# Pattern stage of a graph network: three settle groups instead of two, a task order by kind, candidates' rows gathered and turned, lone nodes' rows gathered per group

## The chip, the cores and the metric

The kernel runs on one core of a Trainium2 chip. TensorE (PE) does matmuls and transposes, VectorE (DVE) and ScalarE (ACT) elementwise work, GpSimd (POOL) elementwise work and the indirect gathers; SyncE (SP) issues most plain transfers. The metric is the device time of one execution in microseconds (us), lower is better. Shown is the median of three timed runs; beside them one profiled execution, from which all durations below come.

## The reference, cut to what matters

Sixteen graphs of N = 1024 nodes with F = 128 features pass four layers. Layer 0 is an attention over the nonzero entries of each graph's adjacency matrix. Layer 1 thins the adjacency first and then runs three convolutions with batch normalisation; layers 2 and 3 are dense products with the whole adjacency. Each layer adds its input and is layer-normalised. The change concerns the thinning of layer 1, which is a loop over the rows of each graph:

```python
def step(carry, n):
    row = jnp.take(carry, n, axis=0)
    nbi = row.astype(jnp.int32)
    num = jnp.sum(nbi)
    sf = jnp.where(num > T_DIL, (num + K_DIL - 1) // K_DIL, 1)   # T_DIL = 10, K_DIL = 2
    rank = jnp.cumsum(nbi)
    rm = row & (rank % sf == 0)
    valid = (mask_b[n] != 0) & (num > 1)
    rm = jnp.where(valid, rm, False)
    keep = ~rm
    carry = carry.at[n].set(row & keep)
    carry = carry.at[:, n].set(carry[:, n] & keep)
    return (carry, None)
```

A row with at most ten neighbours (when its turn comes) loses all of them; a row with more loses the neighbours whose running rank is a multiple of half their number. What is left is very sparse.

## The kernel before, in words

The program has four phases, one after the other: the attention (`phase_att`, which also writes a 0/1 copy of every adjacency to DRAM, `mask_d`, and the layer's result `x1_d`), the pattern stage (`phase_pattern`), the convolutions (`phase_conv`) and the dense layers (`phase_end`). Only the pattern stage is changed. It replaces the sequential loop by a few matmul passes. For each of the 16 graphs b it runs two generators, and for each half of the graphs a third one; a `yield` divides each into steps.

`find(b)` (L751) loads the graph's mask (2 MB, tile `m`, three buffers, L754) and counts degrees with 64 one-column matmuls (L760). POOL cuts the eight diagonal blocks of the mask (`md`, L767). Three passes `earlier` (L777, L781) tell which nodes keep nothing ("small") and which are candidates; at most 128 candidates get a slot each. `slots` (L713 to L722) makes a one-hot matrix `oh` of nodes by slots, `nodes` (L727 to L733) the node number of each slot and the index of its row in DRAM. POOL gathers the candidates' rows of the adjacency by that index (`rows`, L810: 128 rows of 4 KB). The candidates' columns of the mask come from a product of the whole mask with `oh`: `pg`, 64 matmuls of 128x128 (L823). DVE multiplies `pg` by `stay` into `base` (L831), which a further product ranks (`pr`, L837, `RB`, `num0`). Last, `rows` are transposed (L854), copied (L856) and multiplied with `oh32` (L860) into `V`.

`settle(g)` (L864) works on eight graphs at once. Five rounds follow each other, each with nine small DVE operations (128x8), three wide ones (128x1024, L896 to L898), eight one-column matmuls (L901) and a copy of their result `gone` (L903), on which the next round's first operation depends. Then follow wide operations, three products and a transpose, and a store to `slots_d` (L953).

`alone(b)` (L956) ranks all nodes of one graph against its settled candidates (`prank`, L964), marks hits on ACT and DVE (L970, L972), finds the nodes that are left alone, gives them slots as above, and issues two gathers on POOL: the candidates' rows of x1 (L989, through `rows_of_x1`, L746) and the lone nodes' diagonal entries (L990). After all tasks, `rows_of_x1` gathers the lone nodes' rows of x1 for all 16 graphs (L1006), for which `inner` (L735) makes the indices per half.

`rolling(tasks, 5, 2)` (L635, L1003) interleaves the generators in program order: at most five are active, a new one starts when the last one has made two steps, and only the head of the list may start:

```python
while (todo and len(active) < depth and (not active or active[-1][2] >= lag)
       and all(n in ended for n in todo[0][2])):
```

The list is f0 to f9, s0, then f10, a0, f11, a1 and so on to f15, a5, then s1, a6, a7, and a8 to a15 (f for find, s for settle, a for alone). s0 needs f0 to f7, a0 to a7 need s0, s1 needs f8 to f15, a8 to a15 need s1.

Program order is not quite the order of execution: a planner places each engine's instructions ahead of time, by program order and by its own estimates of when an operand is ready. So an instruction may stand earlier than the program has it (the trace has flag operations of L1024, written after all tasks, at 1708 us). [...]

PSUM holds two wide buffers (tag `pb`, shared by `pg`, `pt`, `py`, `pk`, `prank`) and four small ones (tag `ps`).

Of the kernel before, what the change touches and what calls it, by code (L numbers as in the profile page):

```python
# [10 lines left out]
F32 = mybir.dt.float32  # L11
F32R = mybir.dt.float32r
BF16 = mybir.dt.bfloat16
F16 = mybir.dt.float16
# [3 lines left out]
ALU = mybir.AluOpType  # L18
# [4 lines left out]
B, N, F = 16, 1024, 128  # L23
P = 128
T = N // P
# [75 lines left out]
EDGE = 256.0  # L101
# [512 lines left out]

KEEP = 10
ROUNDS = 5
HALF = B // 2


# [12 lines left out]
    arrays["q_one_up"] = np.ascontiguousarray(np.broadcast_to(node[:P], (P, P)))  # L632


def rolling(tasks, depth, lag):  # L635


    todo, active, ended = list(tasks), [], set()
    while todo or active:
        while (  # L640
            todo and len(active) < depth and (not active or active[-1][2] >= lag)
            and all(n in ended for n in todo[0][2])
        ):
            active.append([todo[0][0], todo[0][1], 0])
            todo.pop(0)
        for a in list(active):
            try:
                next(a[1])
                a[2] += 1
            except StopIteration:  # L650
                active.remove(a)
                ended.add(a[0])
# [3 lines left out]
def phase_pattern(ctx, tc, t, c, mask_d, slots_d, x1_d, keep, flags):  # L656
# [78 lines left out]
    def inner(k0, k1):  # L735

        k = slice(k0, k1)
        at = sm.tile([P, HALF], F32, name="at")
        none = sm.tile([P, HALF], F32, name="none")
        nc.vector.tensor_scalar(at, keep.node[:, k], -1.0, 0.0, op0=ALU.add, op1=ALU.max)  # L740
        nc.vector.tensor_scalar(none, keep.node[:, k], 0.0, float(N), op0=ALU.is_equal, op1=ALU.mult)
        nc.vector.tensor_copy(keep.inner[:, k], at)
        nc.vector.tensor_tensor(keep.row[:, k], at, none, ALU.add)

    def rows_of_x1(k):
        nc.gpsimd.indirect_dma_start(  # L746
            keep.xs[:, k, :], None, x1_d[k % B],
            bass.IndirectOffsetOnAxis(ap=keep.inner[:, k : k + 1], axis=0),
        )

    def find(b):  # L751
# [60 lines left out]
            bass.IndirectOffsetOnAxis(ap=keep.index[:, b : b + 1], axis=0),  # L812
        )

        le = wp.tile([P, T, P], F16, name="le", bufs=3)
        for ti in range(T):
            nc.scalar.activation(le[:, ti, :], row, AF.Sign, bias=half_up[:, ti : ti + 1])
# [1 line left out]

        pg = ps_b.tile([P, T, P], F32, name="pg", tag="pb")  # L820
        for ni in range(T):
            for ci in range(T):
                nc.tensor.matmul(  # L823
                    pg[:, ni, :], m[:, ci, ni * P : (ni + 1) * P], oh[:, ci, :],
                    start=ci == 0, stop=ci == T - 1,
                )
        late = sm.tile([P, T], F16, name="late")
        nc.vector.scalar_tensor_tensor(late, cand, 2.0 * N, node_col, op0=ALU.mult, op1=ALU.add)
        stay = wp.tile([P, T, P], F16, name="stay")
# [33 lines left out]

    def settle(g):  # L864

        bs = slice(g * HALF, (g + 1) * HALF)
        shape = [P, HALF, P]

        def tiny(name):
            return sm.tile([P, HALF], F32, name=name, bufs=3)  # L870

        def wide(name, dtype=F16):
            return lp.tile(shape, dtype, name=name)

        def spread(x):
            return x.unsqueeze(2).to_broadcast(shape)

        gone = tiny("gone")
        nc.vector.memset(gone, 0.0)
        rb = RB[:, bs, :]  # L880
        for k in range(ROUNDS):
            num, h, big, top = tiny("num"), tiny("h"), tiny("big"), tiny("top")
            nc.vector.scalar_tensor_tensor(num, num0[:, bs], 1.0, gone, op0=ALU.add, op1=ALU.subtract)

            nc.vector.tensor_scalar(h, num, 0.5, 0.25, op0=ALU.mult, op1=ALU.add)
            nc.vector.tensor_scalar(h, h, ROUND, None, op0=ALU.add)
            nc.vector.tensor_scalar(h, h, ROUND, None, op0=ALU.subtract)
            nc.vector.tensor_scalar(big, num, float(KEEP), None, op0=ALU.is_gt)


            nc.vector.scalar_tensor_tensor(v1[:, bs], h, EDGE - 1, gone, op0=ALU.add, op1=ALU.add)
            nc.vector.tensor_tensor(top, v1[:, bs], h, ALU.add)
            nc.vector.scalar_tensor_tensor(top, top, -EDGE, big, op0=ALU.add, op1=ALU.mult)
            nc.vector.tensor_scalar(v2[:, bs], top, EDGE, None, op0=ALU.add)
            e1, e2, rm = wide("e1"), wide("e2"), wide("rm")
            nc.vector.tensor_tensor(e1, rb, spread(v1[:, bs]), ALU.is_equal)  # L896
            nc.vector.tensor_tensor(e2, rb, spread(v2[:, bs]), ALU.is_ge)
            nc.vector.tensor_tensor(rm, e1, e2, ALU.max)  # L898
            pn = ps_s.tile([P, HALF], F32, name="pn", tag="ps")
            for j in range(HALF):  # L900
                nc.tensor.matmul(pn[:, j : j + 1], rm[:, j, :], one, start=True, stop=True)  # L901
# [5 lines left out]
        inner(g * HALF, (g + 1) * HALF)  # L907
# [8 lines left out]
        for j in range(HALF):  # L916
# [15 lines left out]
        nc.vector.scalar_tensor_tensor(k1, num, 1.0, k1, op0=ALU.is_le, op1=ALU.max)  # L932
# [3 lines left out]
        for j in range(HALF):  # L936
# [12 lines left out]
        pt = ps_b.tile(shape, F32, name="pt", tag="pb")  # L949
        for j in range(HALF):  # L950
# [42 lines left out]
        )  # L993
        yield

    tasks = [(f"f{b}", find(b), []) for b in range(HALF + 2)]
    tasks.append(("s0", settle(0), [f"f{b}" for b in range(HALF)]))
    for b in range(HALF - 2):
        tasks += [(f"f{HALF + 2 + b}", find(HALF + 2 + b), []), (f"a{b}", alone(b), ["s0"])]
    tasks.append(("s1", settle(1), [f"f{b}" for b in range(HALF, B)]))  # L1000
    tasks += [(f"a{b}", alone(b), ["s0"]) for b in (HALF - 2, HALF - 1)]
    tasks += [(f"a{b}", alone(b), ["s1"]) for b in range(HALF, B)]
    rolling(tasks, 5, 2)  # L1003
    inner(B, B + HALF)
    inner(B + HALF, 2 * B)
    for k in range(B, 2 * B):  # L1006
        rows_of_x1(k)


    nc.vector.tensor_scalar(keep.lone, keep.lone, 1.0, None, op0=ALU.min)  # L1010

# [1202 lines left out]
```

## Time and profile before

| | |
|---|---|
| median of three runs | 3212.45 us (3210.42 to 3214.26) |
| profiled execution | 3201.61 us, span 3199.7 us |
| PE busy over the span | 2800.9 us (88%) |
| DVE busy | 2251.8 us (70%) |
| ACT busy | 1778.9 us (56%) |
| POOL busy | 1271.8 us (40%) |
| mean granted TensorE clock | 0.922 |
| pattern stage in the trace | about 1690 to 2083 us |

Busy time is the time in which an engine had an instruction in execution; matmul ends are modelled, so a busy PE is not a PE at its peak. The pattern stage lies between the last work of the attention (POOL's L531 at 1689.4 us) and the last product of the last `alone` (L728 at 2082.1 us). The span is cut into stretches below, with the busy time of every engine in each; in such a table the number behind an engine's busy time is its count of instructions, and PEclk is the granted clock.

### The profile page before, as it was taken

What the parts mean: (1) busy time and instruction counts of PE and PEld (TensorE: products, weight loads), DVE (VectorE), ACT (ScalarE), POOL (GpSimd) and SP (SyncE); (2) the same over time, 40 slices, a digit from 0 to 9 for tenths busy, and PEclk for the clock granted to TensorE, in tenths of its full rate; (3) what the DMA queues carried; (4) which work ended last, traced back from release to release, by engine and by line L of the source; (5) the groups of instructions that cost most, each with busy time, mean ns of one, the idle gap of its engine ahead of it and who ended that gap; (6) DMA issues with size and microseconds to landing.
All of it is one profiled execution on the core that took longest, in us unless ns stands there. A gap on an engine that the chain in (4) does not pass through costs nothing. (4 is left out here: it accounts for less than half of the span.)

```text
span 3199.7 us, 70693 instructions
## 1 busy us (share of the span) xinstructions
PE 2800.9 (88%) x25724; PEld 2487.4 (78%) x25724; DVE 2251.8 (70%) x8226; ACT 1778.9 (56%) x5608; POOL 1271.8 (40%) x1280
## 2 busy tenths in 40 slices
PE   6999999999999999999996968477786899999997
PEld 3877877778777877788886858266676899999997
DVE  5878878788788878788774466746555566666665
ACT  3867777777776777777772323145645233333342
POOL 5645555454545454453113423243423223333221
PEclk8999999999999999999996878688988899999999
DMA  6422332223322332222023532044444434444441
GB/s 179 116 66 79 85 99 79 65 79 99 92 63 80 94 99 75 69 78 72 21 92 115 188 108 93 16 161 143 149 171 151 161 130 156 174 159 168 158 146 30
DMA packets 162023, 348.62 MB, mean 109 GB/s; under 512 B 14708, under 2 KB 68230, under 8 KB 161536
## 3 DMA queue, kind: packets, MB, share of 16 engines
q1 hardware_dynamic: 149760, 311.37, 30.6%
q0 software_dynamic: 10752, 28.42, 3.1%
q10 hardware_dynamic: 1152, 4.19, 0.5%
q8 instruction: 206, 3.38, 0.4%
q14 instruction: 153, 1.25, 0.1%
HBM read 257.87 MB, written 87.03 MB: 108 GB/s over the span
## 5 line engine op out<-in xcount | busy, mean ns | idle before, releaser
L272 POOL TENSOR_SCALAR mask<-ld 104x1024 f16<-104x1024 f32 (+1 forms) x150 | 443.2, 2955 | 548.1 <-PE pw L354 236.1
L434 PE MATMUL pg<-parts,oh 104*128 104x384 f32 (+1 forms) x1760 | 539.0, 382 | 49.7 <-ACT hg L452 49.1
L465 PE MATMUL pa<-hg,we 128*104 128x129 f32 (+1 forms) x3520 | 569.4, 277 | 1.8
L446 DVE SCALAR_TENSOR_TENSOR junk<-pg,w_a 128x128 f32<-128x128 f32 x1600 | 405.2, 283 | 173.3 <-PE pg L439 170.1
L465 PEld LDWEIGHTS pa<-hg,we 128*104 128x104 f32 x3520 | 498.0, 175 | 32.8 <-ACT hg L452 19.6
L452 ACT ACTIVATE hg<-pg,hg 128x128 f32<-128x128 f32 x1600 | 509.8, 370 | 17.1
L439 PE MATMUL pg<-parts,oh 104*128 104x384 f32 (+1 forms) x1760 | 473.2, 343 | 0.0
L434 PEld LDWEIGHTS pg<-parts,oh 104*128 104x128 f32 x1760 | 282.2, 193 | 78.4 <-ACT hg L452 62.0
L439 PEld LDWEIGHTS pg<-parts,oh 104*128 104x128 f32 x1760 | 314.6, 193 | 0.0
L450 ACT ACTIVATE hg<-sc 128x2 f32<-128x2 f32 (+1 forms) x880 | 188.6, 216 | 168.6 <-DVE junk L446 163.2
L419 DVE TENSOR_TENSOR we<-k_id,ids 128x832 f32<-128x832 f16 (+1 forms) x240 | 228.5, 952 | 8.5 <-PE pa L465 4.7
L1343 POOL TENSOR_TENSOR rstd<-ve,mhalf 128x4 f32<-128x4 f32 x96 | 97.0, 1010 | 323.9 <-DVE ve L1342 323.8
L389 ACT CAST oh<-oh_b 104x1024 fp32r<-104x1024 bf16 (+1 forms) x240 | 221.3, 977 | 1.9 <-DVE oh_b L385 1.7
L291 PE MATMUL pw<-w_all,xT 128*104 128x512 f32 x320 | 185.6, 664 | 17.0 <-DMA xT<-in_xTp 8.3
L1347 DVE TENSOR_SCALAR x<-x,mv,rstd 128x128 f32<-128x128 f32 x256 | 104.7, 449 | 92.6 <-POOL rstd L1343 92.6
L385 DVE TENSOR_TENSOR oh_b<-pw,k_slot_edge 104x512 bf16<-104x512 f32 (+1 forms) x240 | 144.6, 635 | 9.6 <-PE pw L384 7.1
L357 ACT CAST qs<-pw 104x416 f16<-104x416 f32 (+1 forms) x240 | 114.4, 477 | 66.4 <-PE pw L354 62.7
L364 DVE SCALAR_TENSOR_TENSOR one_way<-qs,mask 104x1040 bf16<-104x1040 f16 (+9 forms) x160 | 150.4, 940 | 0.1
L500 POOL TENSOR_TENSOR own<-parts 104x128 f32<-104x128 f32 x160 | 96.9, 637 | 118.4 <-DVE x_rows L521 82.4
L1452 ACT ACTIVATE y<-x,shift,rstd 128x128 f32<-128x128 f32 x128 | 52.7, 482 | 162.9 <-POOL shift L1445 162.9
L378 ACT CAST oh_b<-pw 104x512 bf16<-104x512 f32 (+1 forms) x240 | 133.1, 556 | 13.6 <-PE pw L377 13.5
L336 DVE TENSOR_TENSOR g<-k_slot,off 105x1408 f16<-105x1408 f16 x80 | 131.9, 1649 | 11.5 <-ACT off L332 11.4
(356 smaller groups left out, 6662.0 us busy)
## 6 DMA issues: line engine op xcount, KB each, us to landing
ld<-in_adjT SPq DMA_DIRECT2D x135, 416.0 KB
m<-mask_d SPq DMA_DIRECT2D x16, 2048.0 KB
keep_adj<-in_adjT SPq DMA_DIRECT2D x8, 4096.0 KB
adj<-in_adjT SPq DMA_DIRECT2D x8, 4096.0 KB
mask_d<-mask SPq DMA_DIRECT2D x144, 208.0 KB
hT_d<-uT SPq DMA_DIRECT2D x48, 512.0 KB
h<-hT_d SPq DMA_DIRECT2D x48, 512.0 KB
hT<-hT_d SPq DMA_DIRECT2D x32, 512.0 KB
```

What stands on the lines that cost most here:

```text
L272: engine.tensor_scalar(mt[:n, s, :N], ld[:n], 0.0, None, op0=ALU.is_gt)
L291: nc.tensor.matmul(pw[:W], xT[:, s * W : (s + 1) * W], w_all, start=True, stop=False, skip_group_check=True)
L364: nc.vector.scalar_tensor_tensor(junk[:W, :nb, :], q[:W, at : at + nb, :W], EDGE, mt[:W, i, i * W : NP].rearrange("p (n w) -> p n w", w=W) ...
L385: nc.vector.tensor_tensor(o[:W, n0 : n0 + m, 1, :], pw[:W, :m, :], k_slot_edge[:W].unsqueeze(1).to_broadcast([W, m, C]), ALU.is_equal,)
L389: nc.scalar.copy(wide.ends[:W, n0 : n0 + m], o[:W, n0 : n0 + m])
L419: nc.vector.tensor_tensor(we[:, :n, :], k_id.unsqueeze(1).to_broadcast([P, n, W]), wide.ids[:, 2 * lo : 2 * hi].unsqueeze(2).to_broadcast( ...
L434: nc.tensor.matmul(flat[:, first : 3 * F], own, d.parts[i][:W, p, first:], start=p == 0, stop=False, skip_group_check=True,)
L439: nc.tensor.matmul(pg[:, 1::step, :], other, reversed_parts(d.parts[j][:W, p, :], step), start=False, stop=p == 1, skip_group_check=True,)
L446: nc.vector.scalar_tensor_tensor(junk, pg[:, 1 + e, :], 0.0, w_a2, op0=ALU.max, op1=ALU.mult, accum_out=d.sc[:, at + e : at + e + 1],)
L450: nc.scalar.activation(hg[:, u - lo, :ways, F], d.sc[:, at : at + ways], AF.Exp)
L452: nc.scalar.activation(hg[:, u - lo, e, :F], pg[:, 3 - 3 * e, :], AF.Copy, scale=hg[:, u - lo, e, F : F + 1])
L465: nc.tensor.matmul(PA[bank][:W, at : at + part.stop - part.start], we[:, 2 * (u - lo) + e, :], hg[:, u - lo, e, part], start=False, stop=T ...
```

## The change

Five edits, all in the pattern stage.

1. The groups of `settle` are 0 to 5, 6 to 11 and 12 to 15, where there were 0 to 7 and 8 to 15; its tiles shrink from eight to six or four graphs, and `settle` runs three times.
2. `rolling` starts tasks by kind: up to four finds, one settle and two of the kind "alone" are active at once, each kind with a lag of two steps among its own, and any task of the list whose predecessors have ended may start, not only the head.
3. The candidates' columns of the mask: a second gather on POOL fetches the candidates' rows of `mask_d` (128 rows of 2 KB, tile `marks`); `pg` becomes eight matmuls that turn them (with a diagonal matrix `there`, one small DVE operation, which also blanks unused slots). The mask is symmetric without its diagonal, so rows and columns agree.
4. The small operations of a round fall from nine to seven; one more stands after the rounds.
5. The lone nodes' rows of x1 are gathered in three tasks `lone_rows(g)`, each after the six, six or four `alone` of its group, in place of one block after all tasks.

```diff
+GROUPS = ((0, 6), (6, 12), (12, 16))
...
-def rolling(tasks, depth, lag):
+def rolling(tasks, most, lag):
...
-        while (
-            todo and len(active) < depth and (not active or active[-1][2] >= lag)
-            and all(n in ended for n in todo[0][2])
-        ):
-            active.append([todo[0][0], todo[0][1], 0])
-            todo.pop(0)
+        for task in list(todo):
+            name, kind, steps, after = task
+            same = [a for a in active if a[1] == kind]
+            if len(same) < most[kind] and (not same or same[-1][3] >= lag) and ended.issuperset(after):
+                active.append([name, kind, steps, 0])
+                todo.remove(task)
...
+        marks = wp.tile([P, N], F16, name="marks")
+        nc.gpsimd.indirect_dma_start(
+            marks, None, mask_d.rearrange("b n m -> (b n) m"),
+            bass.IndirectOffsetOnAxis(ap=keep.index[:, b : b + 1], axis=0),
+        )
+
+        there = sm.tile([P, P], F16, name="there")
+        nc.vector.tensor_scalar(there, same, keep.node[:, b : b + 1], 1.0, op0=ALU.mult, op1=ALU.min)
...
         for ni in range(T):
-            for ci in range(T):
-                nc.tensor.matmul(
-                    pg[:, ni, :], m[:, ci, ni * P : (ni + 1) * P], oh[:, ci, :],
-                    start=ci == 0, stop=ci == T - 1,
-                )
+            nc.tensor.matmul(pg[:, ni, :], marks[:, ni * P : (ni + 1) * P], there, start=True, stop=True)
...
-            nc.vector.scalar_tensor_tensor(num, num0[:, bs], 1.0, gone, op0=ALU.add, op1=ALU.subtract)
-
-            nc.vector.tensor_scalar(h, num, 0.5, 0.25, op0=ALU.mult, op1=ALU.add)
-            nc.vector.tensor_scalar(h, h, ROUND, None, op0=ALU.add)
-            nc.vector.tensor_scalar(h, h, ROUND, None, op0=ALU.subtract)
-            nc.vector.tensor_scalar(big, num, float(KEEP), None, op0=ALU.is_gt)
-
-
-            nc.vector.scalar_tensor_tensor(v1[:, bs], h, EDGE - 1, gone, op0=ALU.add, op1=ALU.add)
-            nc.vector.tensor_tensor(top, v1[:, bs], h, ALU.add)
+
+            nc.vector.scalar_tensor_tensor(num, num0[:, bs], 1.5, gone, op0=ALU.add, op1=ALU.subtract)
+            nc.vector.tensor_scalar(h, num, 0.5, ROUND, op0=ALU.mult, op1=ALU.add)
+            nc.vector.tensor_scalar(big, num, KEEP + 0.5, None, op0=ALU.is_gt)
+
+
+            nc.vector.scalar_tensor_tensor(v1[:, bs], h, EDGE - 1 - ROUND, gone, op0=ALU.add, op1=ALU.add)
+            nc.vector.scalar_tensor_tensor(top, h, -ROUND, v1[:, bs], op0=ALU.add, op1=ALU.add)
...
-    tasks = [(f"f{b}", find(b), []) for b in range(HALF + 2)]
-    tasks.append(("s0", settle(0), [f"f{b}" for b in range(HALF)]))
-    for b in range(HALF - 2):
-        tasks += [(f"f{HALF + 2 + b}", find(HALF + 2 + b), []), (f"a{b}", alone(b), ["s0"])]
-    tasks.append(("s1", settle(1), [f"f{b}" for b in range(HALF, B)]))
-    tasks += [(f"a{b}", alone(b), ["s0"]) for b in (HALF - 2, HALF - 1)]
-    tasks += [(f"a{b}", alone(b), ["s1"]) for b in range(HALF, B)]
-    rolling(tasks, 5, 2)
-    inner(B, B + HALF)
-    inner(B + HALF, 2 * B)
-    for k in range(B, 2 * B):
-        rows_of_x1(k)
-
+    def lone_rows(g):
+        b0, b1 = GROUPS[g]
+        inner(B + b0, B + b1)
+        for k in range(B + b0, B + b1):
+            rows_of_x1(k)
+        yield
+
+    tasks = [(f"f{b}", "find", find(b), []) for b in range(B)]
+    for g, (b0, b1) in enumerate(GROUPS):
+        tasks.append((f"s{g}", "settle", settle(g), [f"f{b}" for b in range(b0, b1)]))
+        tasks += [(f"a{b}", "alone", alone(b), [f"s{g}"]) for b in range(b0, b1)]
+        tasks.append((f"x{g}", "alone", lone_rows(g), [f"a{b}" for b in range(b0, b1)]))
+    rolling(tasks, {"find": 4, "settle": 1, "alone": 2}, 2)
```

The rest of the diff passes the width of the group (`b1 - b0`) where `HALF` stood, and takes the constant `ROUND` off `h` once after the rounds.

More of the change, by code (lines that the diff above doesn't have):

```diff
@@ L632, in pattern_constants @@
     arrays["q_one_up"] = np.ascontiguousarray(np.broadcast_to(node[:P], (P, P)))
-def rolling(tasks, depth, lag):
+def rolling(tasks, most, lag):
     todo, active, ended = list(tasks), [], set()
     while todo or active:
-        while (
-            todo and len(active) < depth and (not active or active[-1][2] >= lag)
-            and all(n in ended for n in todo[0][2])
-        ):
-            active.append([todo[0][0], todo[0][1], 0])
-            todo.pop(0)
+        for task in list(todo):
[4 more added lines that the diff above has]
+                todo.remove(task)
         for a in list(active):
             try:
-                next(a[1])
-                a[2] += 1
+                next(a[2])
+                a[3] += 1
             except StopIteration:
@@ L737, in inner @@
         k = slice(k0, k1)
-        at = sm.tile([P, HALF], F32, name="at")
-        none = sm.tile([P, HALF], F32, name="none")
+        at = sm.tile([P, k1 - k0], F32, name="at")
+        none = sm.tile([P, k1 - k0], F32, name="none")
         nc.vector.tensor_scalar(at, keep.node[:, k], -1.0, 0.0, op0=ALU.add, op1=ALU.max)
@@ L864, in settle @@
     def settle(g):
-        bs = slice(g * HALF, (g + 1) * HALF)
-        shape = [P, HALF, P]
+        b0, b1 = GROUPS[g]
+        bs, n = slice(b0, b1), b1 - b0
+        shape = [P, n, P]
         def tiny(name):
-            return sm.tile([P, HALF], F32, name=name, bufs=3)
+            return sm.tile([P, n], F32, name=name, bufs=3)
         def wide(name, dtype=F16):
@@ L898, in settle @@
             nc.vector.tensor_tensor(rm, e1, e2, ALU.max)
-            pn = ps_s.tile([P, HALF], F32, name="pn", tag="ps")
-            for j in range(HALF):
+            pn = ps_s.tile([P, n], F32, name="pn", tag="ps")
+            for j in range(n):
                 nc.tensor.matmul(pn[:, j : j + 1], rm[:, j, :], one, start=True, stop=True)
@@ L906, in settle @@
         nc.vector.tensor_scalar(below[:, bs], v2[:, bs], -0.5, None, op0=ALU.add)
-        inner(g * HALF, (g + 1) * HALF)
+        nc.vector.tensor_scalar(h, h, -ROUND, None, op0=ALU.add)
+        inner(b0, b1)
         up = wide("up")
@@ L915, in settle @@
         py = ps_b.tile(shape, F32, name="py", tag="pb")
-        for j in range(HALF):
+        for j in range(n):
             nc.tensor.matmul(py[:, j, :], up[:, j, :], run[:, :P], start=True, stop=True)
@@ L931, in settle @@
         nc.vector.tensor_tensor(k1, k1, big, ALU.mult)
-        nc.vector.scalar_tensor_tensor(k1, num, 1.0, k1, op0=ALU.is_le, op1=ALU.max)
+        nc.vector.scalar_tensor_tensor(k1, num, 1.5, k1, op0=ALU.is_le, op1=ALU.max)
         own = wide("own")
@@ L935, in settle @@
         pk = ps_b.tile(shape, F32, name="pk", tag="pb")
-        for j in range(HALF):
+        for j in range(n):
             nc.tensor.matmul(pk[:, j, :], same, low[:, j, :], start=True, stop=False)
@@ L949, in settle @@
         pt = ps_b.tile(shape, F32, name="pt", tag="pb")
-        for j in range(HALF):
+        for j in range(n):
             nc.tensor.transpose(pt[:, j, :], d[:, j, :], c.ident)
@@ L994, in alone @@
         yield
-    tasks = [(f"f{b}", find(b), []) for b in range(HALF + 2)]
-    tasks.append(("s0", settle(0), [f"f{b}" for b in range(HALF)]))
-    for b in range(HALF - 2):
-        tasks += [(f"f{HALF + 2 + b}", find(HALF + 2 + b), []), (f"a{b}", alone(b), ["s0"])]
-    tasks.append(("s1", settle(1), [f"f{b}" for b in range(HALF, B)]))
-    tasks += [(f"a{b}", alone(b), ["s0"]) for b in (HALF - 2, HALF - 1)]
-    tasks += [(f"a{b}", alone(b), ["s1"]) for b in range(HALF, B)]
-    rolling(tasks, 5, 2)
-    inner(B, B + HALF)
-    inner(B + HALF, 2 * B)
-    for k in range(B, 2 * B):
-        rows_of_x1(k)
+    def lone_rows(g):
+        b0, b1 = GROUPS[g]
+        inner(B + b0, B + b1)
[8 more added lines that the diff above has]
+    rolling(tasks, {"find": 4, "settle": 1, "alone": 2}, 2)
     nc.vector.tensor_scalar(keep.lone, keep.lone, 1.0, None, op0=ALU.min)
```

## The prediction

> **What bounds the kernel now.** I read the page first. The chain that ended last reaches back only to about 2379 us, behind the pattern stage, so it says nothing of it. I therefore cut the stage into stretches at the places where its character changes, and asked for the busy time of each engine:
>
> ```profile
> core 0: us, PE busy (x) PEld busy (x) DVE busy (x) ACT busy (x) POOL busy (x), PEclk, DMA share, GB/s
> 1690.00:1858.00 168.00, 140.67 (x2861) 137.02 (x2862) 77.62 (x205) 50.88 (x141) 70.87 (x122) 0.75 0.52 167
> 1858.00:1898.00 40.00, 16.04 (x279) 14.96 (x278) 33.85 (x89) 3.75 (x10) 3.73 (x9) 0.55 0.07 24
> 1898.00:1997.00 99.00, 88.38 (x1697) 80.08 (x1697) 56.56 (x143) 36.70 (x90) 29.66 (x41) 0.90 0.33 106
> 1997.00:2046.00 49.00, 16.19 (x159) 12.32 (x159) 40.10 (x114) 3.80 (x6) 12.70 (x13) 0.57 0.06 14
> 2046.00:2083.00 37.00, 23.84 (x246) 14.12 (x244) 26.33 (x68) 10.14 (x18) 7.76 (x9) 0.82 0.06 19
> 2083.00:2095.00 12.00, 3.01 (x12) 2.78 (x13) 3.21 (x15) 0.92 (x2) 8.53 (x9) 0.50 0.88 282
> ```
>
> The stage alternates between two bounds. In the first and third stretch (finds; finds with six alones) PE is busy 84% and 89%, DVE 46% and 57%. In the second and fourth (the two settles) PE is busy 40% and 33%, and DVE, at 85% and 82%, follows a chain from round to round. The fifth holds the eight last alones, the sixth the handover to the convolutions. From 1690 to 2083 (393 us) PE has 285.1 us of work and DVE 234.5: neither fills the time.
>
> Next the groups by shape from 1690 to 2100, for the operations the change touches, then that stretch's list of waits:
>
> ```profile
> L823 PE MATMUL pg<-oh,m 128*128 128x128 f16 x1024 | 67.9, 233 | 1.6 <-DVE oh L719 1.6
> L767 POOL TENSOR_TENSOR md<-m,q_less 128x128 f16<-128x128 f16 x128 | 59.7, 501 | 52.4 <-DMA m<-mask_d 52.2
> L810 POOL DMA_INDIRECT rows<-in_adj,keep_index x16 | 21.8, 1359 | 78.1 <-issue 38.9 <-PE pu L781 33.6 <-DVE keep_index L731 5.6
> ```
>
> ```profile
> POOL md L767 <- DMA m<-mask_d: 52.2, 10, 15.5
> ...
> PE pn L901 <- DVE rm L898: 36.6, 8, 6.2
> ...
> PE pt L854 <- DMA rows<-in_adj,keep_index: 14.6, 8, 3.1
> ```
>
> `pg` is PE's largest item, 67.9 us. PE waits 36.6 us for settle rounds. POOL stands 52.2 us for mask loads, because in the old kernel a mask buffer is held until `pg` has read it. The issue queue of SP shows the pitch of a find:
>
> ```profile
> 1722.72 129.36 SPq L754 DMA_DIRECT2D m<-mask_d  x10
> ```
>
> Ten loads start over 129.36 us, so 14.4 us lie between two finds. From 1858 on nothing new starts until s0 has ended: a0 heads the list and waits for it.
>
> [...] `rows` lands after a median of 4.7 us (4.3 to 6.8). [...] while `md` ran at 1862.0 to 1865.6, settle's small operations took 0.35 to 0.41 us, otherwise 0.17. [...] the settle stretches show 0.55 and 0.57, the third stretch 0.90. Filling those holes should not cost clock.
>
> **The change part by part.**
>
> *Columns by gather (edit 3).* PE loses 1024 matmuls of 67.9 us, 66 ns each in a row, and gains 128: 8.5 us. PE's work falls from 285.1 to 225.7. DVE gains 16 `there`, by the nearest rows (L689, L691: 0.18 and 0.41 us) 3 to 7 us; I take 3. POOL gains 16 gathers; `rows` takes 1.36 us on POOL, so 21.8 us, no bound beside POOL's 125 of 393 us. The DMA engines move 2.9 instead of 2.6 MB per find; at the 287 GB/s seen at 1660 to 1680 us, 10 us, below the old pitch. Gain: a mask buffer comes free after the third `earlier`, so loads start sooner and POOL's 52.2 us of waiting shrinks. The new wait: `pg` waits for a gather that waits for the node numbers. From index to landing I count 1.36 (`rows`) + 1.36 (`marks`) + 4.7 = 7.4 us; ahead of it may stand another find's `md` (59.7/16 = 3.7 us). Behind `pg` on PE stand the other finds' passes, and settle's and alone's products. One step of three other finds covers some 2.3 us of PE (a find will have 8.3 us in eleven steps, below). For `rows`, with two steps more of cover, PE waited only 14.6 us in all, as the planner put other work ahead. For `marks` I bound the loss at 0 to 5 us per find and take 1.5; part falls into time in which PE has nothing else to do.
>
> *Three groups (edits 1, 4).* The elements stay. Per settle there were about 69 small operations (45 in rounds), now 60; three times 60 against twice 69 is 42 more at 0.17, +7 us. There are 24 wide operations per settle; from 1.22 us at 1024 elements and 0.35 at 128 (L840) the fixed part is about 0.2 us, so +4 us with a third settle. DVE: 234.5 + 3 + 7 + 4 = 248.
>
> *Order by kind (edit 2).* It takes away the head of the list that blocks. Finds go on while s0 and s1 run, so DVE's settle rounds and PE's find passes lie beside each other. It moves every find's `rows` and mask load past settle, on POOL and SP; I price that as the utilisation below.
>
> *Lone rows per group (edit 5).* The last eight gathers ran at 2084 to 2094 us, 1.25 us each, beside the handover, in which PE waited 9.3 us for weights and not for them. So moving them gains nothing. The cover lost: six of them stand in POOL's queue for 7.5 us ahead of some find's gathers, two times; at worst 15 us, I take 2 inside the utilisation.
>
> *The sum.* PE per find: 140.67 us over 168/14.4 = 11.7 finds, 12.0 us; less 59.4/16 = 3.7, it is 8.3. At the 84% that PE reached in the first stretch this gives a pitch of 10 us, with the DMA's 10 us just as tight; I take 10.5. f0 ended at 1748.7 us (its `V` copy); f5 then ends near 1801. By then DVE has done about eight finds' work (six whole, four begun) at 7.8 us (the rows of one find, mean durations summed, and `there`) and 4 us of constants, 66 us. There remain 182 us, and PE's 226 - 8 x 8.3 = 160. DVE is now the larger load. If DVE is busy 80% of the rest (between the 71% of the last alones and the 89% of PE in the third stretch, near the settles' 82 and 85%), 182/0.80 = 227 us, and the stage ends at 2028 instead of 2083: 55 us less. A check on another way: even at the old pitch of 14.4 us, f15 would end at 1749 + 15 x 14.4 = 1965; a settle of four graphs (five rounds of about 3.7 us and 9 us behind them, 27 us) and four alones (37/8 = 4.6 us each, 18) bring 2010. So the overlap pays most, and DVE limits. Handover and later phases stay. The profiled execution, 3201.6 us, would become 3146.6; the median shown lies 10.8 us above it, so 3157 us.
>
> **The rivals.**
>
> *A, smaller gain.* DVE reaches only 71%, as in the fifth stretch, where it waits for ACT and PE in turns, and `marks` costs its waits. 182/0.71 = 256 us, an end at 2057, 26 us less: 3186. For it: two engines almost equally loaded and queues in a fixed order. Against it: three kinds of independent tasks.
>
> *B, larger gain.* DVE reaches PE's 89%: 204 us, an end at 2005, 78 us less: 3134. For it: that stretch had only two kinds of task and reached 89%.
>
> *C, slower.* The wait for `marks` takes the place of `pg`'s work. POOL places a later find's `md`, which waits for its mask (up to 15.5 us before), ahead of `marks`; PE stands at `pg`, and since `base` needs `pg`, DVE stands too. With 5 us uncovered in each of 16 finds that is 80 us against the 55: 25 us slower, 3237. It decides from 55/16 = 3.4 us per find in which both engines are idle. Against it: POOL's waits for masks shrink with earlier loads, and the old holes of 89 us in settle are there to be filled.
>
> *D, no change.* The planner's own estimates place the tasks much as before, so the blocks stay, and the saved matmuls become idle time: 3212. Against it: in the old order nothing was there to place while s0 ran.
>
> **How the numbers follow.** Likeliest case 0.45, its own range 3142 to 3172; A 0.22, B 0.20, C 0.08, D 0.05. The range 3120 to 3203 leaves out C, D and the far end of B. Within 0.2% (6.4 us) is about what a measurement of this kernel can't tell from no change. Faster 0.87, same 0.05, slower 0.08.
>
> **What would show it.** Right: 128 `pg` matmuls at some 8 to 9 us; the first convolution products near 2035 instead of 2092; no stretch of 40 us with PE below 50% before the last settle; DVE near 248 us in the stage; a pitch of mask loads of 10 to 12 us. Wrong: PE waiting for `marks` for more than 50 us in all, POOL waiting for masks as long as before, or the last settle and its alones taking over 60 us after the last find. The forecast fails most easily through the 80%, which I only place between measured shares.

## The result and the profile after

| | before | after |
|---|---|---|
| median, runs on one chip | 3213.36 us | 3214.61 us |
| ratio | | 1.0006 (0.9989 to 1.0024) |
| profiled execution, span | 3201.61, 3199.7 us | 3215.12, 3212.9 us |
| mean granted TensorE clock | 0.922 | 0.911 |
| pattern stage | 1689.4 to 2083.0: 393.6 us | 1688.0 to 2091.6: 403.6 us |

The change makes no difference that can be measured; 55 us less were forecast. The stage is counted here, and in all runs below, from the start of the attention's last operation on POOL (L531) to the start of the convolutions' load of `slots_w` on SP. The profiled execution of before lies 12 us below its median here, so the 10 us between the two stages are a reading of two single executions; the ratio is the verdict.

First the busy time of the engines in the stage of after, cut at the same times as before's, with the whole stage last:

```profile
core 0: us, PE busy (x) PEld busy (x) DVE busy (x) ACT busy (x) POOL busy (x), PEclk, DMA share, GB/s
1690.00:1858.00 168.00, 106.73 (x2051) 101.78 (x2052) 74.11 (x202) 41.66 (x116) 72.72 (x118) 0.59 0.45 152
1858.00:1898.00 40.00, 25.36 (x565) 24.46 (x564) 28.50 (x84) 9.14 (x26) 14.36 (x20) 0.54 0.55 183
1898.00:1997.00 99.00, 75.74 (x1214) 64.46 (x1212) 65.69 (x195) 31.77 (x79) 32.45 (x44) 0.69 0.30 97
1997.00:2046.00 49.00, 26.50 (x245) 19.45 (x244) 37.62 (x120) 12.02 (x24) 15.26 (x15) 0.78 0.14 41
1688.00:2091.60 403.60, 262.72 (x4338) 227.20 (x4338) 239.22 (x702) 104.58 (x263) 152.32 (x211) 0.65 0.34 112
```

The holes of the two settles (second and fourth stretch: PE 40% and 33% before) are filled only to 63% and 54%. What was gained there is lost in the first stretch, the finds: PE is busy 64% of it where it was 84%, DVE does no more than before (74 and 78 us), and the granted clock is 0.59 instead of 0.75. Nothing replaces PE as the bound there.

Next after's groups by shape from 1690 to 2100 us, and below them one group of before that was not shown:

```profile
L832 PE MATMUL pg<-there,marks 128*128 128x128 f16 x128 | 15.2, 292 | 54.3 <-DMA marks<-mask_d,keep_index 54.3
L818 POOL DMA_INDIRECT marks<-mask_d,keep_index x16 | 19.5, 1216 | 4.9 <-issue 4.6 <-PE pn L906 0.3
L866 PE MATMUL pv<-oh,turned 128*128 128x128 f32 x256 | 52.9, 384 | 7.9 <-ACT turned L862 7.8
```

```profile
L860 PE MATMUL pv<-oh,turned 128*128 128x128 f32 x256 | 40.4, 322 | 0.0
```

The 1024 `pg` matmuls are 128 now, but 54.3 us of waiting stand before them, and matmuls that the change leaves alone are dearer: those of `pv` cost 52.9 us instead of 40.4. The list of waits of the same stretch names who stands still (us in all, times, longest):

```profile
DVE base L837 <- PE pg L832: 62.9, 14, 9.3
PE pg L832 <- DMA marks<-mask_d,keep_index: 54.3, 15, 6.2
PE pn L906 <- DVE rm L903: 32.6, 11, 4.4
POOL md L769 <- DMA m<-mask_d: 24.1, 5, 7.9
```

In 15 of 16 finds PE waits for the gather, and in 14 DVE waits at `base` for the same find: both engines are idle at once. The timelines of POOL, SP's queue and PE show one find (start, duration, and in brackets the idle time before):

```profile
1731.57 1.88 POOL L812 DMA_INDIRECT rows<-in_adj,keep_index  x1 [8.09 <-DVE there L824]
1733.75 1.57 POOL L818 DMA_INDIRECT marks<-mask_d,keep_index  x1 [0.30 <-issue]
1735.34 3.27 POOL L769 TENSOR_TENSOR md<-m,q_less 128x128 f16<-128x128 f16 x8
```

```profile
1731.86 0.36 SPq L756 DMA_DIRECT2D m<-mask_d  x1
```

```profile
1734.70 2.50 PE L866 MATMUL pv<-oh,turned 128*128 128x128 f32 x10 [0.68 <-ACT turned L862]
1743.02 1.03 PE L832 MATMUL pg<-there,marks 128*128 128x128 f16 x8 [5.82 <-DMA marks<-mask_d,keep_index]
1743.85 1.59 PE L866 MATMUL pv<-oh,turned 128*128 128x128 f32 x6
```

POOL issues at once: `rows`, 0.30 us later `marks`, and only then the next find's `md`. From the start of `rows` to the first `pg` it takes 11.45 us, 5.82 of which PE stands still; in the next find 11.30 (1749.58 to 1760.88). Behind `pg` stands work that is ready: of the sixteen `pv` matmuls of an earlier find ten run before the wait and six right after it. PE kept its order: the six, whose operands were there, stood 5.82 us behind `pg`.

The SP line shows what the gathers meet: a mask load of 2 MB, issued 0.29 us after `rows`. With edit 3 the third `earlier` of a find frees its mask buffer. Another find's last matmul of that pass on its mask ends at 1731.78, and the load starts at 1731.86, beside this find's gathers. In eight of the sixteen finds a load starts within 3 us of `rows`, and `marks` takes 7.5 to 9.6 us from issue to `pg`; in the other eight it lands in 3.9 to 4.9 us, as in the fourth find here:

```profile
1768.76 0.95 POOL L818 DMA_INDIRECT marks<-mask_d,keep_index  x1 [0.30 <-issue]
1772.75 1.03 PE L832 MATMUL pg<-there,marks 128*128 128x128 f16 x8 [3.18 <-DMA marks<-mask_d,keep_index]
```

Of PE's 54.3 us of waiting, 38.1 lie in the eight finds with a load beside the gathers. Before, a load started within 3 us of `rows` in three finds, each time 0.7 us or more after it, and the longest landing of `rows` on record is 6.8 us; in after it is 10.4.

The mask loads don't come faster: twelve start over 198.61 us, 18 us apart (14.4 before).

PE's account of the stage: busy 285.1 before, 262.7 after; idle 108.5 and 140.9. The `pg` matmuls give back 52.7 us (67.9 less 15.2). All other matmuls rise from 217.2 to 247.5, 30.3 us more. Of the idle time 54.3 are new at `marks`, the old 14.6 at `rows` are gone, and the rest falls by 7.3. Together -52.7 + 30.3 + 32.4 = +10.0 us, the difference of the stages.

### The profile page after: what moved, and what is told of

Same layout as the page of the kernel before. It is cut to its first block, busy times and chain, and to the rows that moved or that the text cites. A ratio compares the mean times of both kernels' runs of the same rounds, so it can differ in the third digit from the quotient of the medians.

```text
span 3212.9 us, 69006 instructions
## 1 busy us (share of the span) xinstructions
PE 2776.5 (86%) x24828; PEld 2453.3 (76%) x24828; DVE 2256.3 (70%) x8312; ACT 1777.3 (55%) x5609; POOL 1292.1 (40%) x1296
## 5 line engine op out<-in xcount | busy, mean ns | idle before, releaser
L357 ACT CAST qs<-pw 104x416 f16<-104x416 f32 (+1 forms) x240 | 114.4, 477 | 67.3 <-PE pw L354 63.6
L1458 ACT ACTIVATE y<-x,shift,rstd 128x128 f32<-128x128 f32 x128 | 52.7, 482 | 163.0 <-POOL shift L1451 163.0
```

## The experiments

My theory after seeing this: the gather of edit 3 pays out what the order gains, because the planner puts `pg` too early for it; the low clock follows from those waits. The rivals: that the order by kind is itself worth little (then undoing edit 3 leaves the time as it is), and that the gather's transfer is simply too slow beside the mask loads. A ratio below is to the runs of before of its own group; where two groups are compared, it is by these ratios.

### One part alone

The first four runs share the runs of before, 3222.73 us. `m_pg` is after with edit 3 undone:

```diff
-        marks = wp.tile(...); nc.gpsimd.indirect_dma_start(marks, ...); there = ...
-            nc.tensor.matmul(pg[:, ni, :], marks[:, ni * P : (ni + 1) * P], there, start=True, stop=True)
+            for ci in range(T):
+                nc.tensor.matmul(pg[:, ni, :], m[:, ci, ni * P : (ni + 1) * P], oh[:, ci, :],
+                                 start=ci == 0, stop=ci == T - 1)
```

> The changed kernel with the columns taken from the mask again (64 matmuls per graph, no gather of marks); groups, order by kind, fewer small operations and lone rows per group stay. Theory W (the wait of pg for its gather eats what the rest brings): the waits of 54 us at pg go, 59 us of matmuls come back, which partly lie in time PE had idle; the overlap of settle with finds remains and shows: 3165 to 3195 us, faster than both. Theory O (the order by kind itself costs, as it puts all kinds into one queue and runs finds at a longer pitch): 3215 to 3260 us, no better than before or slower.

`gather_only` is before with edit 3 alone; for room, two tiles of `settle` share buffers with two others:

```diff
+        marks = wp.tile(...); nc.gpsimd.indirect_dma_start(marks, ...); there = ...
+            nc.tensor.matmul(pg[:, ni, :], marks[:, ni * P : (ni + 1) * P], there, start=True, stop=True)
...
-        up = wide("up")
+        up = wide("own")
...
-        y1, y2, low = wide("e1"), wide("e2"), wide("low")
+        y1, y2, low = wide("e1"), wide("e2"), wide("rm")
```

> The kernel before with edit 3 alone: candidates' rows of the mask gathered and turned, old order, two groups (two of settle's wide tiles share buffers so that it fits). Theory W: pg waits for marks also here, 3 to 4 us per find; 59 us of matmuls go and about as much waiting comes: 3200 to 3225 us. Theory O: the gather is good by itself and the order spoils it: 3160 to 3185 us.

`plain_marks` is after with a transfer of the same size that waits for no index. It leaves out the choice of rows, and shares the same buffers in `settle` as `gather_only`:

```diff
+        marks = mp.tile([P, N], F16, name="marks", bufs=4)
+        nc.sync.dma_start(marks, mask_d[b, :P, :])
...
-        marks = wp.tile([P, N], F16, name="marks")
-        nc.gpsimd.indirect_dma_start(marks, ...)
```

> The changed kernel, but marks is filled by a plain load of the first 128 rows of the mask, issued by SP with the find's mask, so pg waits for no gather and POOL issues 16 fewer; it leaves out the choice of rows (two of settle's wide tiles share buffers so that it fits). Theory W: the 54 us of waiting and part of the low TensorE clock go: 3140 to 3175 us. Theory O: pg's wait only covered time in which PE would have been idle anyway: 3200 to 3220 us.

`later2` is after with `pg` two steps later in program order:

```diff
+        yield
+        yield
         pg = ps_b.tile([P, T, P], F32, name="pg", tag="pb")
```

> The changed kernel with two more steps between the gather of marks and pg, so that the planner sets more of the other finds' work ahead of pg on PE. Theory W: most of the 54 us of waiting at pg goes, finds get two steps longer: 3165 to 3195 us. Theory O: 3205 to 3230 us.

| run | median | ratio (95%) | stage | PE waits for `marks` |
|---|---|---|---|---|
| `m_pg` | 3207.57 | 0.9957 (0.9944 to 0.997) | 391.3 | none |
| `gather_only` | 3260.75 | 1.012 (1.01 to 1.0141) | 440.9 | 76.6 us |
| `plain_marks` | 3190.27 | 0.9897 (0.9878 to 0.9917) | 394.4 | none |
| `later2` | 3187.95 | 0.9902 (0.9882 to 0.9923) | 372.7 | 20.1 us |

The whole stage of `m_pg`, `gather_only` and `later2`, one line of the busy times by stretch from each:

```profile
1693.30:2084.60 391.30, 299.26 (x5234) 264.26 (x5234) 233.52 (x686) 105.25 (x263) 127.61 (x196) 0.74 0.33 105
```

```profile
1691.40:2132.30 440.90, 264.88 (x4338) 231.23 (x4338) 242.12 (x632) 105.64 (x262) 144.57 (x207) 0.64 0.31 102
```

```profile
1688.40:2061.10 372.70, 247.01 (x4338) 215.55 (x4338) 244.32 (x702) 105.58 (x263) 155.04 (x211) 0.66 0.37 121
```

And a wait of `gather_only`, then two of `later2`:

```profile
PE pg L830 <- DMA marks<-mask_d,keep_index: 76.6, 15, 7.3
```

```profile
PE pn L909 <- DVE rm L906: 39.0, 12, 5.5
PE pg L835 <- DMA marks<-mask_d,keep_index: 20.1, 10, 5.1
```

Edit 3 alone costs 1.2%, some 38 us: the wait of 76.6 us is more than the matmuls it saves. (The shared buffers weren't measured by themselves.) The other edits without it, `m_pg`, gain 0.43%, 14 us of the 55, less than the first theory expected and more than its rival. With `pg` two steps later the wait falls by 34 us and the stage by 31, on the same instructions, though seven of its finds still have a mask load beside the gathers. So a later `pg` covers most of the slow landing. The two `yield`s also lengthen every find by two steps, and `m_pg` with them was not run, so not all of the gain is shown to be the wait's. `plain_marks` doesn't measure the wait: its tile in the mask pool makes the first mask loads of the stage start at 1707 instead of 1661 us, and the phases behind the stage got shorter too, 14 us against before, with the other rows; its stage is no shorter than that of before.

### How much is the wait, how much the matmuls

These four share 3215.86 us. `swap` issues the `marks` gather ahead of `rows`; `both` is after with the 64 old matmuls run too, and overwritten by the eight new ones; `later2_two` is `later2` with two groups, and settle's buffers shared as in `gather_only`; `swap_later2` joins two of the edits.

```diff
 swap
-        rows = wp.tile(...); nc.gpsimd.indirect_dma_start(rows, ...)
         marks = wp.tile(...); nc.gpsimd.indirect_dma_start(marks, ...)
+        rows = wp.tile(...); nc.gpsimd.indirect_dma_start(rows, ...)
 both
+        for ni in range(T):
+            for ci in range(T):
+                nc.tensor.matmul(pg[:, ni, :], m[:, ci, ni * P : (ni + 1) * P], oh[:, ci, :],
+                                 start=ci == 0, stop=ci == T - 1)
         for ni in range(T):
             nc.tensor.matmul(pg[:, ni, :], marks[:, ni * P : (ni + 1) * P], there, start=True, stop=True)
 later2_two
-GROUPS = ((0, 6), (6, 12), (12, 16))
+GROUPS = ((0, 8), (8, 16))
```

> The changed kernel with the gather of marks issued ahead of that of rows. If the wait at pg is mostly the gather's own path (queue on POOL, then its landing behind 512 KB of rows), marks is there 1.4 to 3 us sooner: the 54 us of waiting at pg fall to 15 to 35 us and the time to 0.985 to 0.995 of the kernel before. If pg waits because POOL issues late (POOL held up by md or an earlier wait), the order of the two makes no difference: 0.998 to 1.003.

> The changed kernel, but the 64 old matmuls of pg run as well, into the same PSUM tile, before the eight new ones overwrite it: PE does the 59 us of work again, without using it. If the wait for marks took the very place of the matmuls (PE had nothing else at that point), the work fits into the wait [...]: 0.99 to 1.008 of the kernel before. If the wait lies in time in which PE had slack anyway and the work matters, it adds most of its 59 us: 1.012 to 1.02.

> The kernel with two more steps before pg, with two groups of eight in place of three (two of settle's wide tiles share buffers so that it fits). If three groups help by starting settle earlier and leaving a short tail, it is slower than with three: 0.994 to 1.003 of the kernel before. If the groups don't matter beside the wait for marks: 0.987 to 0.993 as with three.

> Both remedies: marks first, and two steps more before pg. If the wait at pg is what keeps the kernel from its forecast, the 20 us of it that are left with two more steps go too: 0.980 to 0.988 of the kernel before. If DVE's fixed order sets the rest, no more than with the two steps: 0.988 to 0.992.

| run | median | ratio (95%) | stage | PE waits for `marks` |
|---|---|---|---|---|
| `swap` | 3206.59 | 0.9972 (0.9961 to 0.9983) | 384.5 | 57.7 us |
| `both` | 3236.41 | 1.0056 (1.0038 to 1.0075) | 424.0 | 39.5 us |
| `later2_two` | 3184.76 | 0.9905 (0.9888 to 0.9921) | 374.9 | 40.0 us |
| `swap_later2` | 3188.91 | 0.9917 (0.99 to 0.9933) | 365.2 | 25.3 us |

`m_pg`, `both` and after split edit 3 in two. `both` against `m_pg` (same old matmuls, the gather added): 0.99%, 32 us, the price of the gather and its wait. After against `both` (the old matmuls taken away): 0.50%, 16 us, for 1024 instructions and 68 to 73 us of PE. That is a net: in `both` a mask buffer is held until the old matmuls have read it, so only four of its finds have a mask load beside the gathers, where after has eight. What the matmuls alone are worth isn't settled by the pair.

Of `swap` these are the waits:

```profile
PE pg L832 <- DMA marks<-mask_d,keep_index: 57.7, 15, 7.8
DVE base L837 <- PE pg L832: 44.4, 15, 6.7
```

The gather is issued earlier, and PE waits as long as before. So `pg` has moved forward with it, which fits a planner that expects a gather sooner than it lands; its estimates themselves aren't in the trace. Why the run is still 0.34% faster than after isn't settled; DVE waits 18.5 us less at `base`. With `later2` the swap brings nothing more. Two groups do as well as three: `later2_two` and `later2` agree, though PE waits 20 us longer for `marks`, so beside `later2` edit 1 has no effect that can be measured.

### Later still, and in the old order

These share 3223.15 us. `old_later2` is `gather_only` with the two `yield`s (shown as `later2` above); `later4` has four; `later2_f5` allows five finds at once; `both_later2` is `both` with the two `yield`s.

```diff
 later2_f5
-    rolling(tasks, {"find": 4, "settle": 1, "alone": 2}, 2)
+    rolling(tasks, {"find": 5, "settle": 1, "alone": 2}, 2)
```

> The kernel before with the gather alone (edit 3) and two more steps before pg; old order, two groups. With the gather alone it stood at 1.012 of the kernel before. If the order by kind is worth what the difference of gather_only and the changed kernel says (about 1.1%), it stays 1% behind the kernel with the new order and two steps: 0.998 to 1.005. If the order by kind helped only because it covered the wait, the two steps bring the old order to 0.988 to 0.995 as well.

> The kernel with two more steps before pg and five finds active in place of four. If too few finds in flight keep DVE at 70%: 0.978 to 0.986 of the kernel before. If DVE's load and order set it: 0.988 to 0.994; three mask buffers and three of oh may hold the fifth back.

> The changed kernel with four more steps before pg in place of two. If every us of waiting at pg counts: the 20 us left with two steps fall below 10 and the time to 0.983 to 0.989. If the wait is no longer what binds: 0.989 to 0.996, since a find gets longer.

> The kernel with two more steps before pg, and the 64 old matmuls run as well and are overwritten. If PE is off the path there (DVE binds), its 59 us of extra work cost at most 15 us: 0.990 to 0.995. If PE still binds together with DVE: 30 to 59 us, 1.000 to 1.009.

| run | median | ratio (95%) | stage | PE waits for `marks` |
|---|---|---|---|---|
| `old_later2` | 3229.53 | 1.0019 (1.001 to 1.0028) | 412.6 | 53.4 us |
| `later2_f5` | 3194.11 | 0.9914 (0.9895 to 0.9933) | 382.1 | 24.0 us |
| `later4` | 3197.07 | 0.9924 (0.9905 to 0.9943) | 376.8 | 26.4 us |
| `both_later2` | 3244.07 | 1.0068 (1.0041 to 1.0094) | 433.8 | 6.0 us |

The two `yield`s gain 1.0% in the old order as well, as in the new one (1.0%). With the gather, the other four edits, the order by kind among them, are worth 1.1 to 1.2% (1.012 to 1.0006; 1.0019 to 0.9902), without it 0.43%: part of what they do seems to be to cover a wait that edit 3 brings (76.6 us in `gather_only`, 54.3 in after). Four `yield`s wait no less than two, and more finds at once bring nothing. `both_later2` can't be read as meant. Its waits show why:

```profile
POOL md L769 <- DMA m<-mask_d: 104.2, 11, 23.0
```

The late `pg` holds the mask buffers, and POOL waits 104.2 us for the next masks.

### The spacing of finds

A list of the last copy of each find (`V`) in after shows that finds end in fours. The gap between the fourth and the fifth is 35 us, between the eighth and the ninth 38:

```profile
1769.60 0.27 ACT L867 COPY v_all<-pv 128x128 f32<-128x128 f32 x1
1784.04 0.27 ACT L867 COPY v_all<-pv 128x128 f32<-128x128 f32 x1 [3.46 <-PE pv L866]
1819.45 0.27 ACT L867 COPY v_all<-pv 128x128 f32<-128x128 f32 x1 [9.69 <-PE pv L866]
...
1860.58 0.27 ACT L867 COPY v_all<-pv 128x128 f32<-128x128 f32 x1 [6.03 <-PE pv L866]
1898.97 0.27 ACT L867 COPY v_all<-pv 128x128 f32<-128x128 f32 x1 [3.87 <-PE pv L866]
```

With a lag of two steps and a limit of four, finds of eleven steps, which a twelfth call ends, start in steps 0, 2, 4, 6, and the fifth only in step 12. A lag of three gives 0, 3, 6, 9, 12, wholly even; with the 13 steps of `later2` it gives 0, 3, 6, 9, 14. (The expectations below count this fifth start one step early.) Before has such bunches too, of five, with a gap of 33 us behind the first. The last four runs share 3213.67 us and change the lag, which holds for settle and alone as well, or the limit:

```diff
 after_lag3, m_pg_lag3, later2_lag3
-    rolling(tasks, {"find": 4, "settle": 1, "alone": 2}, 2)
+    rolling(tasks, {"find": 4, "settle": 1, "alone": 2}, 3)
 after_f6
-    rolling(tasks, {"find": 4, "settle": 1, "alone": 2}, 2)
+    rolling(tasks, {"find": 6, "settle": 1, "alone": 2}, 2)
```

> The changed kernel with a lag of three (starts at 0, 3, 6, 9, 11). Even spacing also sets more of other finds' steps between gather and pg. If bunching matters: 0.985 to 0.995 of the kernel before. If not: 0.998 to 1.004.

> The changed kernel with the columns from the mask (no gather of marks) and a lag of three. Without the lag it stood at 0.9957 of the kernel before. If bunching matters: 0.982 to 0.992. If PE's load sets it: 0.993 to 0.999.

> The kernel with two more steps before pg and a lag of three steps in place of two between tasks of a kind, so four finds of 13 steps follow at 0, 3, 6, 9, 13. If the bunching of finds keeps the engines at 70%: 0.974 to 0.985 of the kernel before, and the last copies of V come evenly. If a plain limit of DVE and PE: 0.988 to 0.994.

> The changed kernel with six finds active, lag two (starts at 0, 2, 4, 6, 8, 10, 11: even). More finds in flight give pg more cover, as far as the three buffers of masks and of oh allow. If bunching matters: 0.985 to 0.996 of the kernel before. If not: 0.999 to 1.005.

| run | median | ratio (95%) | stage | PE waits for `marks` |
|---|---|---|---|---|
| `after_lag3` | 3195.16 | 0.9946 (0.9924 to 0.9967) | 380.8 | 34.9 us |
| `m_pg_lag3` | 3178.41 | 0.9891 (0.9862 to 0.9919) | 364.7 | none |
| `later2_lag3` | 3199.26 | 0.9963 (0.9946 to 0.998) | 386.6 | 26.1 us |
| `after_f6` | 3222.97 | 1.0026 (1.0013 to 1.004) | 406.9 | 70.9 us |

The same copies in `m_pg_lag3` are 16 us apart (the largest gap is 29 us, in `m_pg` 49), and its stage has a clock of 0.74:

```profile
1775.85 0.27 ACT L863 COPY v_all<-pv 128x128 f32<-128x128 f32 x1 [0.96 <-PE pv L862]
1792.86 0.27 ACT L863 COPY v_all<-pv 128x128 f32<-128x128 f32 x1 [2.40 <-PE pv L862]
1808.66 0.27 ACT L863 COPY v_all<-pv 128x128 f32<-128x128 f32 x1 [1.20 <-PE pv L862]
```

```profile
1691.40:2056.10 364.70, 300.87 (x5234) 269.59 (x5234) 238.09 (x686) 104.81 (x263) 131.95 (x194) 0.74 0.36 113
```

The lag of three gains 0.66% without the gather (0.9957 to 0.9891). Then PE is busy 82% of the stage, with all the old matmuls, and POOL waits 21.5 us for masks where it waited 68.0 in `m_pg`. With the gather it gains 0.60%, but there two things change at once: the starts are even, and the wait for `marks` falls from 54.3 to 34.9 us, with a mask load within 3 us of `rows` in only two finds. `after_f6` separates them in part. Its finds end evenly too, the first five 16 to 17 us apart, but in twelve of them a mask load starts beside the gathers, `marks` waits 70.9 us, and nothing is gained. So with the gather even starts alone aren't enough; without it one run shows a gain. On `later2` the lag loses 0.6%; that is not explained, and the two gains don't add. The best versions beat both kernels by about 1%, equal within their intervals: `later2` (with `later2_two`), and `m_pg_lag3`, which has no gather of columns at all.

## Why the prediction was wrong

The forecast had the stage end at 2028 us, and it ended at 2091.6: 63.6 us, in the two parts of the sum. The sixth find (f5) was to end near 1801 us and ended at 1837, 36 us late. From there 182 us of DVE's work at 80% were to take 227 us; this is that stretch in after:

```profile
1837.00:2091.60 254.60, 171.25 (x2576) 140.18 (x2574) 177.83 (x541) 69.19 (x164) 83.42 (x100) 0.69 0.25 80
```

The work was as forecast (177.8 us), but DVE is busy 70% of 254.6 us, 27.6 more.

**The 36 us: "For `marks` I bound the loss at 0 to 5 us per find and take 1.5."** It measured 54.3 us in 15 finds, 3.6 us each, with both engines idle: inside the bounds, but at the end that I gave 8%. Rival C put the point from which it decides at 3.4 us per find, and there the gain was gone. More than 50 us of waiting was the sign that the prediction set for itself. By 1837 us PE had waited 36.5 us for `marks`, in seven finds. With most of the wait taken away, in `later2`, f5 ends at 1806.5 us. Two terms under the 1.5 were off.

The first is the landing. The sum of 7.4 us took the 4.7 of `rows` before over to `marks`; it also counts the issue of `marks` twice, as a landing is measured from the start of the issue. From the start of `rows` to `pg` after takes 5.5 to 7.1 us in the eight finds without a mask load beside the gathers, and 8.8 to 11.5 in the eight with one. The prediction names the sooner start of loads as a gain; it doesn't see that the sooner load starts with the gather. (No run kept the loads off the gathers and changed nothing else; that they slow the landing rests on the split by finds, eight and eight in after, twelve, at 8.4 to 9.8 us, and four, at 4.1 to 6.0, in `after_f6`.) The shortest landing of `marks` in after is 3.9 us, the longest 9.6.

The second is the cover. "The planner put other work ahead" was carried over from `rows`, which has two steps more. For `marks` it doesn't hold, as `later2` shows. The size is that of C, but not its cause: no `md` stands ahead of `marks` on POOL.

**The 27.6 us: "If DVE is busy 80% of the rest".** The 70% is rival A's figure. `later2`, with little wait left, has 185.8 us in 254.6, 73%: so most of this part isn't the wait's. `m_pg` has 69%, and `m_pg_lag3`, with even starts, 75%. I took the limit from the load of one engine; a find is a chain through all of them, and the fours in which finds end leave gaps that I didn't see, though the lag and the limit in the diff were enough to work them out. How much of the missing 10% is these gaps isn't shown: even starts bring 75%, not 80. The pitch took the saved matmuls in full, 3.7 us per find; taking them out brought 16 us in all, from `both` to after. The check by the old pitch of 14.4 us failed as well: the pitch of mask loads became 18.

**"Filling those holes should not cost clock" was wrong too.** It was my estimate; the clocks of before beside it (0.55 and 0.57 in the settles, 0.90 in the third stretch) don't show it. The clock of the stage fell from 0.75 to 0.65, and the matmuls that stayed took 30.3 us more. I looked at the settles' holes and not at the finds, where the clock was 0.59 instead of 0.75, beside waits for `marks` of up to 6.2 us. But my theory that the clock follows from these waits doesn't hold over the runs. `plain_marks` has no such wait, and its clock and matmuls are those of after:

```profile
1692.00:2086.40 394.40, 260.47 (x4355) 226.99 (x4355) 248.27 (x713) 107.29 (x266) 132.34 (x195) 0.64 0.41 136
```

Its matmuls but `pg` took 246.6 us; they took 217.2 before and 225.9 in `m_pg`. What goes with the clock is the old matmuls: the five kernels that run them (before, `m_pg`, `both`, `both_later2`, `m_pg_lag3`) have 0.71 to 0.75 in the stage, with waits for `marks` of 0 to 39.5 us; the thirteen without have 0.63 to 0.69, with 0 to 76.6 us. So the low clock goes with the thinner stream of work rather than with this wait; why was not tested. What it costs varies: 227.7 us of other matmuls in `swap_later2`, 232.6 in `later2`, 249.8 in `after_f6`, and 232.2 in `m_pg_lag3` with all the old ones, so waits may still have a part in the 30.3 us. Nor does this price set the time by itself: `after_lag3` has 248.0 us of other matmuls, as after has, and is 0.6% faster.

A smaller reading was too broad: beside `md`, five of seven small operations of settle took 0.35 to 0.41 us, and two stayed at 0.16 and 0.17. No sum rests on it.

**What held.** DVE's work in the stage, 239.2 us against 248. POOL's gathers of `marks`, 19.5 us, by the price of `rows`. POOL's waits for masks fell from 52.2 to 24.1 us, as buffers come free sooner (1.1 us in `gather_only`, 68.0 in `m_pg`, which keeps the old `pg`). The 128 `pg` matmuls took 15.2 us instead of 8.5: a group of eight took 0.62 us at best, which would be 9.9 in all, and mostly 1.03. No wait of PE's for the lone nodes' rows is in the list; edit 5 was not run by itself.

## What to carry to other kernels

A gather that replaces matmuls must be priced at the place where its consumer stands in its engine's queue: ask what the planner believes of its landing, and if in doubt put the consumer some steps later by hand. When an edit frees a buffer sooner, ask which transfer then starts, and what it starts beside (here a load of 2 MB within 3 us of the gathers, in the finds in which `marks` took 7.5 to 9.6 us to `pg` and not 3.9 to 4.9). Matmuls taken from a stage that is a chain may be worth only a part of their time (here a net 16 us, from `both` to after, for 68 to 73 us of PE). Look at the clock of those that stay: here it was 0.63 to 0.69 with the thinner stream, 0.71 to 0.75 with the old matmuls. Where tasks are started by a lag and a limit, work out the step of every start: a limit times the lag well below a task's steps makes bunches.

## What the runs showed of the hardware

In after, a gather of 128 rows of 2 KB took 3.9 to 4.9 us from issue to landing where no load of 2 MB started within 3 us of the gathers, and 7.5 to 9.6 us to its consumer where one did (eight finds each). From 1734 to 1743 us, in one of the slow finds, the DMA engines moved 309 GB/s. Gathers of 4 KB rows took a median of 6.4 us, where it was 4.7 before, without the second gather and with fewer loads beside it. Two gathers in a row on POOL had 0.30 us between them. One matmul of `pt` (128x128, f32) took 273 ns at the median before, in `m_pg` and in `later2`, 357 in `m_pg_lag3` and 421 in after: one and the same instruction cost half as much again. (The means are 312 before, 378 in after and 394 in `gather_only`.) Taking 1024 of 5234 matmuls out of the stage went with a granted clock of 0.63 to 0.69, where it was 0.71 to 0.75.
